# A Fourier layer on one core: partitions reordered by channel, its 32-point transforms on halves of the TensorE array

## The chip, the cores and the metric

The kernel runs on one core of one Trainium2 chip. The metric is the device time of one execution in microseconds. Before the change three runs took 3753.52, 3758.2 and 3759.49 us; the median, 3758.2 us, is the time that the change is measured against.

## What is computed

The network has four layers on an input of 4 images, 96 channels, 64 x 64 pixels: a Mamba block with a fusion, a ConvNeXt block, a linear attention with a quantized feed-forward part, and a Fourier mixing with another quantized feed-forward part. The change lies in the Fourier mixing of the fourth layer. For 4 images of 4096 tokens with 96 channels, normalized over the channels, it computes:

```python
h = jnp.einsum('bnc,hc->bnh', x, w1)
h = jax.nn.relu(_bn(h, bn1_gamma, bn1_beta, bn1_mean, bn1_var))
X = jnp.fft.fft(h, axis=1, norm='ortho')
xr = jax.nn.relu(X.real * rd - X.imag * idg + rb)
xi = jax.nn.relu(X.imag * rd + X.real * idg + ib)
y = jnp.fft.ifft(xr + 1j * xi, axis=1, norm='ortho').real
o = jnp.einsum('bnh,ch->bnc', y, w2)
return _bn(o, bn2_gamma, bn2_beta, bn2_mean, bn2_var)
```

`w1` widens 96 channels to 192, the transforms run over the 4096 tokens, `rd` and `idg` are one number per channel, and the caller adds the result to x. All of it is in float32.

## The kernel before

The token sum `t` (96 channels x 16384 tokens) stays in SBUF. The function `fourier` (L1285) splits a transform of 4096 tokens into 128 x 32: token = 32 a + n, with `N1` = 128 values of a and `N2` = 32 values of n. Since the input is real, only 65 of 128 frequencies over a are made (`K1` = 65).

The work is cut into 8 units (4 images, and the lower or upper 96 of the 192 channels), each unit into 4 iterations of 6 groups, a group being 4 channels. So there are 32 iterations (`its`), and a partition index of 128 stands for 32 values of n (or of a frequency) times the 4 channels of a group. Before the change the channel is the fast index of the two: partition = 4 n + channel.

The steps of iteration i, each a function:

- `w1` (L1319): two tokens n at a time, PE multiplies the normalized `h` (taken with a step of 32 tokens, that is 128 bytes) by the weights; ACT writes the result after ReLU into `hh` (L1328, 128x192 elements, in two halves).
- `over_n1` (L1334): PE makes the 128-point transform over a of six groups, with `hh` as stationary operand (L1340). DVE multiplies by the twiddle factors, twice (L1344, into `p0` and `p1`), POOL adds the products into real and imaginary part `f` (L1352, two additions on 128 partitions x 390 elements).
- `over_n2` (L1354): PE makes the 32-point transform over n with four matmuls of 390 columns (L1361 to L1364). The stationary operands are 128x128 matrices that are 32-point cosines and sines for each of the four channels; two matmuls add up in each of the PSUM tiles `xi` and `xr`. DVE multiplies `xi` by the coefficients (`ec`, L1367), ACT multiplies `xr` and adds the bias in twelve pieces (`av`, L1376), POOL adds and subtracts the two (L1379, L1380).
- `fold` (L1382): ReLU by ACT (L1386) and DVE, which also folds the frequencies k and 128 - k (L1391, and L1394 for frequency 64) into `zz`; ACT negates one part (L1397).
- `over_k2` (L1399): PE makes the 32-point transform back, with `zz` as stationary operand, twelve matmuls of 128 columns (L1409, L1410), three groups to a PSUM tile; ACT copies each of the two tiles into `bt` (L1411).
- `row64` (L1416): once per unit, the row of frequency 64, through DRAM into `bt`.
- `over_k1` (L1436) and `w2` (L1448): for a finished unit, per block of four n, PE makes the 128-point transform back (L1444), ACT copies it (`ys`, L1446), PE multiplies by the output weights (L1455), DVE adds the result to `t` (L1459, L1461).
- `norm1`, `norm2` (L1303, L1311): the channel norm of the next image.

The order on PE, DVE, ACT and POOL is the program order (`manual_schedule`, L1464): a loop over j (L1468) runs `over_n1(j)`, part of the norm or of `w1` of the next image, `fold(j-2)`, `over_k1` of a first block, `over_n2(j-1)`, `w2`, `over_k1` of a second block, `over_k2(j-3)`, and `w2`. Each engine takes its instructions in that order and waits for the semaphores of the others. So there are three kinds of iteration: with the norm (first half of an image's unit pair, for the next image), with `w1` (second half), and plain ones (last image). Output blocks start with j = 8. The small PSUM tiles `m` (two) are shared by `norm1`, `norm2`, `w1`, `over_k1`, `w2` and `row64` in turn; `s1`, `xr`, `xi` exist once, `i1` twice.

The constants are made on the host by `_constants` (L1550) and laid out by `_lay_out` (L1603), and loaded by `consts2` (L821) during an earlier layer.

Of the kernel before, what the change touches and what calls it, by code (L numbers as in the profile page):

```python
# [9 lines left out]
F32 = mybir.dt.float32  # L10
# [8 lines left out]
B, C, HW, L = 4, 96, 64, 4096  # L19
# [3 lines left out]
MB = 512  # L23
# [79 lines left out]
class Net:  # L103
# [717 lines left out]
    def consts2(self, wk, small):  # L821
# [81 lines left out]
        self.dft2 = load("dft2", [128, 3 * 128])  # L903
# [381 lines left out]
    def fourier(self, dram, t, h):  # L1285
# [5 lines left out]
        with ExitStack() as ctx:  # L1291
# [3 lines left out]
            nbs, bc, bs = (self.dft2[:, k * 128 : (k + 1) * 128] for k in range(3))  # L1295
# [23 lines left out]
            def w1(b, n):  # L1319

                if n == 0:
                    for half in range(2):
                        hh[2 * b + half] = wk.tile([N1, CG, N2, 4], F32, name="hh", tag="hh", bufs=3)
                ps = misc(N1)[:, : 4 * C].rearrange("p (n c) -> p n c", n=2)
                for d in range(2):
                    nc.tensor.matmul(ps[:, d, :], h[:, n + d :: N2], self.a_w1, start=True, stop=True)  # L1326
                for half in range(2):
                    nc.scalar.activation(  # L1328
                        hh[2 * b + half][:, :, n : n + 2, :].rearrange("p g n c -> p n g c"),
                        ps[:, :, half * C : (half + 1) * C].rearrange("p n (g c) -> p n g c", c=4),  # L1330
                        AF.Relu,
                    )

            def over_n1(i):  # L1334

                u, g = its[i]
                ps = pln.tile([128, 2, MB], F32, name="s1_ps", tag="s1")
                for d in range(G):
                    a = d % 3 * 2 * K1
                    nc.tensor.matmul(ps[:, d // 3, a : a + 2 * K1], hh[u][:, g + d], self.dft1, start=True, stop=True)  # L1340
                pp = []
                for k in range(2):
                    p = wk.tile([128, G, 2, K1], F32, name=f"p{k}", tag=f"p{k}")
                    nc.vector.tensor_mul(  # L1344
                        p.rearrange("p (a g) r k -> p a g (r k)", a=2),
                        ps[:, :, : 6 * K1].rearrange("p a (g k) -> p a g k", g=3),
                        self.twid[:, k : k + 1, None, :].to_broadcast([128, 2, 3, 2 * K1]),
                    )
                    pp.append(p)
                f[i] = wk.tile([128, 2, G, K1], F32, name="f", tag="f", bufs=2)  # L1350
                for r in range(2):
                    nc.gpsimd.tensor_add(f[i][:, r], pp[0][:, :, r, :], pp[1][:, :, 1 - r, :])  # L1352

            def over_n2(i):  # L1354
# [3 lines left out]
                fr, fi = (f[i][:, r].rearrange("p g k -> p (g k)") for r in range(2))  # L1358
                f.pop(i)
                xr, xi = (pln.tile([128, MB], F32, name=f"x{r}_ps", tag=f"x{r}")[:, : G * K1] for r in "ri")  # L1360
                nc.tensor.matmul(xi, bc, fi, start=True, stop=False)  # L1361
                nc.tensor.matmul(xi, nbs, fr, start=False, stop=True)
                nc.tensor.matmul(xr, bc, fr, start=True, stop=False)
                nc.tensor.matmul(xr, bs, fi, start=False, stop=True)  # L1364
# [34 lines left out]
            def over_k2(i):  # L1399

                u, g = its[i]
                z = zz.pop(i)
                if g == 0:
                    bt[u] = wk.tile([N1, N2, C], F32, name="bt", tag="bt", bufs=2)
                for e in range(0, G, 3):
                    ps = pln.tile([N1, 4, 128], F32, name="i1_ps", tag="i1", bufs=2)[:, :3]
                    for d in range(3):
                        zd = z[:, e + d].rearrange("p k m -> p (k m)")
                        nc.tensor.matmul(ps[:, d], zd[:, 64:], bc, start=True, stop=False)  # L1409
                        nc.tensor.matmul(ps[:, d], zd[:, :128], bs, start=False, stop=True)  # L1410
                    nc.scalar.copy(  # L1411
                        bt[u].rearrange("p n (g c) -> p g n c", c=4)[:, g + e : g + e + 3],
                        ps.rearrange("p g (n c) -> p g n c", c=4),
                    )
# [13 lines left out]
            def fetch(k):  # L1428

                g = wk.tile([N1, CG, N2, 4], F32, name="hh", tag="hh", bufs=3)  # L1430
                g = g.rearrange("p g n c -> p (g n c)")[:, : N2 // 2 * N1].rearrange("p (n a) -> p n a", n=N2 // 2)
# [16 lines left out]
            def w2(u, n, kept):  # L1448

                b, half = units[u]  # L1450
                if u < len(units) - 1:
                    ps = misc(C)
                else:
                    ps = pln.tile([N1, 4, 128], F32, name="i1_ps", tag="i1", bufs=2)[:C].rearrange("p n a -> p (n a)")
# [95 lines left out]
def _constants():  # L1550
# [9 lines left out]
    th = 2 * np.pi * np.outer(np.repeat(np.arange(N2), 4), k1) / L  # L1560
# [4 lines left out]
    eye = np.eye(4)  # L1565
    bc, bs = np.kron(np.cos(th), eye), np.kron(np.sin(th), eye)
    dft2 = np.concatenate([-bs, bc, bs], 1)

    th = np.pi * np.outer(2 * m + 1, m) / N2
    dft64 = np.stack([np.kron(np.cos(th), eye), np.kron(-np.sin(th), eye)], 1)  # L1570
# [12 lines left out]
        "dft2": dft2.astype(f32),  # L1583
        "dft64": dft64.astype(f32),
# [18 lines left out]
def _lay_out(i):  # L1603
# [20 lines left out]
    for k, v in (("rd", np.diagonal(a["r"])), ("id", np.diagonal(a["i"])), ("rb", a["rb"]), ("ib", a["ib"])):  # L1624
        v128[k] = np.tile(v.reshape(48, 4).T, (32, 1))
# [56 lines left out]
```

## Time and profile before

| | |
|---|---|
| median of three runs | 3758.2 us (3753.52 to 3759.49) |
| the profiled execution | 3750.98 us, its span 3749.2 us |
| granted TensorE clock, mean | 0.919 of full speed |
| PE busy (matmul) | 3115.1 us, 83% |
| PE weight loads | 1404.9 us, 37% |
| DVE busy | 2981.6 us, 80% |
| ACT busy | 2720.5 us, 73% |
| POOL busy | 2566.7 us, 68% |
| DMA moved | 446.63 MB |

The profile is of one execution. Its times count from the start of the span. PE stands for matmuls, PEld for weight loads, which overlap them; DVE is VectorE, ACT ScalarE, POOL GpSimd. A row of a group gives line, engine, operation, output and inputs with partitions x elements, count, busy time, the mean of one in ns, and the idle time ahead of it with what ended it. A float32 matmul appears as two records (two passes over the array), each with its own weight load. The ends of matmuls are modelled, so their starts are the better measure. In the timeline, a bracket behind a row is the engine's idle time ahead of it and the instruction that ended it. The chain of waits follows the work that ended last back from the end, at each step to what released it or to the instruction before it on its engine; "issue" in it is time in which the engine waited for nothing that the profile shows.

The Fourier layer lies between 3108.2 and 3616.2 us.

### The profile page before, as it was taken

Reading aid. Unit: us, or ns where it says so; the run is one execution under the profiler, and the core shown is the slowest. Engines: PE = TensorE matmul, PEld = TensorE weight load, DVE = VectorE, ACT = ScalarE, POOL = GpSimd, SP = SyncE. Lnnn points to the kernel's source line nnn. Section 1 sums busy time; section 2 is a strip of 40 time slices with the busy share of each in tenths; the row PEclk is TensorE's granted clock in tenths of the full one; section 3 lists DMA queues with packets and bytes.
Section 4 is the critical chain, followed back from the end, with each engine's and each line's share of the span. In section 5 each row is a group of like instructions: output and inputs, shape, how many; then the busy total and the mean of one; then the engine's idle time right before and its main releaser. Section 6 shows DMA issues by size and latency. Waiting matters only on the chain. (4 is left out here: it accounts for less than half of the span.)

```text
span 3749.2 us, 46836 instructions
## 1 busy us (share of the span) xinstructions
PE 3115.1 (83%) x15326; PEld 1404.9 (37%) x15326; DVE 2981.6 (80%) x2644; ACT 2720.5 (73%) x5456; POOL 2566.7 (68%) x922
## 2 busy tenths in 40 slices
PE   7887888788878887887888888657799997999888
PEld 3232223223222322232233233147344435676643
DVE  5999999999999999999999999931662493444649
ACT  6887888888888888888888888541345685656557
POOL 1899989898999899989989998811001174434527
PEclk8999899899989998999999899658899999999999
DMA  7656665666565666666665666376000000011001
GB/s 187 156 152 160 166 161 148 165 160 172 145 170 152 173 149 169 157 157 161 166 165 142 172 157 173 91 214 217 1 0 1 1 1 6 24 35 46 24 11 57
DMA packets 171644, 446.63 MB, mean 119 GB/s; under 512 B 48756, under 2 KB 50750, under 8 KB 168064
## 3 DMA queue, kind: packets, MB, share of 16 engines
q1 hardware_dynamic: 171400, 443.64, 45.7%
q8 instruction: 121, 1.98, 0.2%
q14 instruction: 123, 1.01, 0.1%
HBM read 369.97 MB, written 73.50 MB: 118 GB/s over the span
## 5 line engine op out<-in xcount | busy, mean ns | idle before, releaser
L648 POOL TENSOR_TENSOR hs<-hs,crep 128x2048 f32<-128x2048 f32 x384 | 1601.2, 4185 | 224.2 <-DVE hs L643 176.4
L610 ACT ACTIVATE da<-ddb,nega 128x1024 f32<-128x1024 f32 x576 | 661.5, 1149 | 197.7 <-DMA ddb<-dd 124.3
L643 DVE TENSOR_TENSOR_SCAN hs<-da,state,rep 128x1024 f32<-128x1024 f32 x288 | 669.2, 2338 | 39.6 <-PE rep L594 21.9
L621 POOL TENSOR_TENSOR up<-udb,brep 128x1024 f32<-128x1024 f32 x192 | 453.0, 2360 | 73.1 <-DMA udb<-ud 58.9
L665 PE MATMUL y<-hs,sel_r 128*32 128x512 f32 x3072 | 459.6, 692 | 12.8 <-POOL hs L648 12.3
L599 PE MATMUL rep<-dbl,sel_b 32*128 32x512 f32 x768 | 250.1, 730 | 215.1 <-DVE hs L643 215.0
L507 ACT ACTIVATE uta<-delta,bt 128x192 f32<-128x192 f32 x1024 | 381.1, 446 | 0.0
L287 PE MATMUL ps<-n,w_x 97*64 97x512 f32 x1536 | 353.8, 602 | 13.0 <-ACT xc L411 12.1
L643 DVE TENSOR_TENSOR_SCAN hs<-da,state,u 128x1024 f32<-128x1024 f32 x144 | 338.1, 2348 | 23.9 <-PE y L665 8.2
L643 DVE TENSOR_TENSOR_SCAN hs<-dap,state,up 128x1024 f32<-128x1024 f32 x144 | 335.2, 2328 | 0.5 <-ACT dap L610 0.5
L594 PE MATMUL rep<-ident,uta 128*128 128x128 f32 x1536 | 222.6, 287 | 105.6 <-DVE hs L643 93.2
L594 PEld LDWEIGHTS rep<-ident,uta 128*128 128x128 f32 x1536 | 174.9, 146 | 246.5 <-issue 133.3
L636 DVE TENSOR_TENSOR u<-udb,rep 128x1024 f32<-128x1024 f32 x192 | 235.4, 1226 | 24.8 <-DMA udb<-ud 11.4
L1240 POOL CAST hq<-y 128x1536 fp8e5<-128x1536 f16 x64 | 94.0, 1469 | 218.1 <-issue 122.6
L643 DVE TENSOR_TENSOR_SCAN hs<-da,rep 128x1024 f32<-128x1024 f32 x96 | 217.9, 2282 | 21.2 <-PE rep L594 14.8
L610 ACT ACTIVATE dap<-ddb,nega 128x1024 f32<-128x1024 f32 x192 | 214.8, 1119 | 24.9 <-DVE hs L643 24.4
L636 DVE TENSOR_TENSOR rep<-udb,rep 128x1024 f32<-128x1024 f32 x192 | 232.0, 1208 | 0.0
L287 PEld LDWEIGHTS ps<-n,w_x 97*64 97x64 f32 x1536 | 103.8, 137 | 260.2 <-issue 210.0
L665 PEld LDWEIGHTS y<-hs,sel_r 128*32 128x32 f32 x3072 | 73.7, 118 | 335.2 <-issue 257.7
L599 PEld LDWEIGHTS rep<-dbl,sel_b 32*128 32x128 f32 x768 | 65.8, 205 | 353.6 <-issue 295.2
L658 PE MATMUL y<-xc,dp 128*128 128x512 f32 x192 | 125.7, 743 | 31.3 <-ACT bt L463 31.3
L1379 POOL TENSOR_TENSOR av<-av,ec 128x780 f32<-128x780 f32 x32 | 58.8, 1837 | 133.7 <-ACT av L1376 133.7
(275 smaller groups left out, 6201.3 us busy)
## 6 DMA issues: line engine op xcount, KB each, us to landing
udb<-ud SPq DMA_DIRECT2D x768, 128.0 KB
ddb<-dd SPq DMA_DIRECT2D x768, 128.0 KB
crep<-cd SPq DMA_DIRECT2D x512, 128.0 KB
dd<-delta SPq DMA_DIRECT2D x64, 384.0 KB
band<-in_band SPq DMA_DIRECT2D x24, 1024.0 KB
ud<-delta SPq DMA_DIRECT2D x62, 384.0 KB
brep<-cd SPq DMA_DIRECT2D x128, 128.0 KB
x<-in_x SPq DMA_DIRECT2D x32, 384.0 KB
```

The source lines that it names most:

```text
L287: nc.tensor.matmul(ps[rows], w[:, 64 * p : 64 * p + 64], rhs[:, at.start + shift : at.stop + shift], start=k == 0, stop=k == len(ws) - 1, ...
L507: nc.scalar.mul(m["uta"][:, q, :, 32 * s4 : 32 * s4 + 32].rearrange("t (p j) d -> t p j d", p=3), m["udt"][:, :, q].rearrange("t p (j d) - ...
L594: nc.tensor.transpose(x[:, q * 128 : q * 128 + 128], made[k]["uta"][:, q, 2 * h + j], self.ident)
L599: nc.tensor.matmul(x[:, at], sel_b[rows, g], made[k]["dbl"][rows, at], start=True, stop=True)
L610: nc.scalar.activation(da, made[k]["dd", h, j], AF.Exp, scale=nega[:, col : col + 1])
L621: nc.gpsimd.tensor_mul(up, made[k]["ud", p][:, j], made[k]["brep", GP])
L636: nc.vector.tensor_mul(u, made[k]["ud", h][:, j], x)
L643: nc.vector.tensor_tensor_scan(hs[:, 1:], made[k].pop(("da", t)), u, st, ALU.mult, ALU.add)
L648: nc.gpsimd.tensor_mul(hs[:, :, :T], hs[:, :, 1:], twice(made[k]["crep", g]))
L658: nc.tensor.matmul(y, dp[:, items[k][2], p], made[k]["xc"][:, p], start=True, stop=True)
L665: nc.tensor.matmul(made[k]["y", p][row : row + 32], sel_r, made[k]["hs", p, g][:, j, at], start=False, stop=True, skip_group_check=True,)
L1240: nc.gpsimd.tensor_copy(q, y2, saturate=False)
```

## The change

Partitions are reordered: partition = 32 channel + n instead of 4 n + channel, in the twiddle factors, the coefficients per channel and all transform matrices; `hh` changes from (group, n, channel) to (group, channel, n). With that, the 64 partitions of a channel pair are adjacent. The additions that make `f` put, for each channel pair q, the real part on partitions 0 to 63 and the imaginary part on 64 to 127, so a single matmul of 128 rows and 64 columns makes a real or an imaginary result of a pair: the pair's two results go to the two halves of the output partitions. In `over_k2`, each channel pair is a matmul of 64 rows, and the two pairs write to two PSUM tiles.

```diff
-        self.dft2 = load("dft2", [128, 3 * 128])
+        self.dft2 = load("dft2", [128, 2, 64])
+        self.idft2 = load("idft2", [128, 2, 64])
...
-            nbs, bc, bs = (self.dft2[:, k * 128 : (k + 1) * 128] for k in range(3))
+            bc, bs = (self.idft2[:, k] for k in range(2))
+            parts = [slice(0, 64), slice(64, 128)]
...
-                        hh[2 * b + half] = wk.tile([N1, CG, N2, 4], F32, name="hh", tag="hh", bufs=3)
+                        hh[2 * b + half] = wk.tile([N1, CG, 4, N2], F32, name="hh", tag="hh", bufs=3)
...
                     nc.scalar.activation(
-                        hh[2 * b + half][:, :, n : n + 2, :].rearrange("p g n c -> p n g c"),
-                        ps[:, :, half * C : (half + 1) * C].rearrange("p n (g c) -> p n g c", c=4),
+                        hh[2 * b + half][:, :, :, n : n + 2].rearrange("p g c n -> p n (g c)"),
+                        ps[:, :, half * C : (half + 1) * C],
                         AF.Relu,
                     )
...
-                for r in range(2):
-                    nc.gpsimd.tensor_add(f[i][:, r], pp[0][:, :, r, :], pp[1][:, :, 1 - r, :])
+                for q, rows in enumerate(parts):
+                    for r in range(2):
+                        nc.gpsimd.tensor_add(f[i][parts[r], q], pp[0][rows, :, r, :], pp[1][rows, :, 1 - r, :])
...
-                fr, fi = (f[i][:, r].rearrange("p g k -> p (g k)") for r in range(2))
-                f.pop(i)
+                fs = f.pop(i).rearrange("p q g k -> p q (g k)")
                 xr, xi = (pln.tile([128, MB], F32, name=f"x{r}_ps", tag=f"x{r}")[:, : G * K1] for r in "ri")
-                nc.tensor.matmul(xi, bc, fi, start=True, stop=False)
-                nc.tensor.matmul(xi, nbs, fr, start=False, stop=True)
-                nc.tensor.matmul(xr, bc, fr, start=True, stop=False)
-                nc.tensor.matmul(xr, bs, fi, start=False, stop=True)
+                for r, x in ((1, xi), (0, xr)):
+                    for q, rows in enumerate(parts):
+                        nc.tensor.matmul(
+                            x[rows], self.dft2[:, r], fs[:, q], start=True, stop=True, skip_group_check=True
+                        )
...
-                for e in range(0, G, 3):
-                    ps = pln.tile([N1, 4, 128], F32, name="i1_ps", tag="i1", bufs=2)[:, :3]
-                    for d in range(3):
-                        zd = z[:, e + d].rearrange("p k m -> p (k m)")
-                        nc.tensor.matmul(ps[:, d], zd[:, 64:], bc, start=True, stop=False)
-                        nc.tensor.matmul(ps[:, d], zd[:, :128], bs, start=False, stop=True)
+                ps = [pln.tile([N1, MB], F32, name="i_ps", tag=f"i{q}") for q in range(2)]
+                for d in range(G):
+                    zd = z[:, d].rearrange("p k m -> p (k m)")
+                    for k, m in enumerate((bc, bs)):
+                        for p, rows in zip(ps, parts):
+                            nc.tensor.matmul(
+                                p[:, d * 64 : d * 64 + 64],
+                                zd[rows, 64 - 64 * k : 192 - 64 * k],
+                                m[rows],
+                                start=k == 0,
+                                stop=k == 1,
+                            )
+                for q, p in enumerate(ps):
                     nc.scalar.copy(
-                        bt[u].rearrange("p n (g c) -> p g n c", c=4)[:, g + e : g + e + 3],
-                        ps.rearrange("p g (n c) -> p g n c", c=4),
+                        bt[u].rearrange("p n (g c) -> p g n c", c=4)[:, g : g + G, :, 2 * q : 2 * q + 2],
+                        p[:, : G * 64].rearrange("p (g n c) -> p g n c", g=G, c=2),
                     )
...
-                    ps = pln.tile([N1, 4, 128], F32, name="i1_ps", tag="i1", bufs=2)[:C].rearrange("p n a -> p (n a)")
+                    ps = pln.tile([N1, MB], F32, name="i_ps", tag=f"i{n // 4 % 2}")[:C]
```

On the host the matrices follow the new order:

```diff
-    eye = np.eye(4)
-    bc, bs = np.kron(np.cos(th), eye), np.kron(np.sin(th), eye)
-    dft2 = np.concatenate([-bs, bc, bs], 1)
+    eye = np.eye(2)
+    dc, ds = np.kron(eye, np.cos(th)), np.kron(eye, np.sin(th))
+    dft2 = np.stack([np.concatenate([dc, ds]), np.concatenate([-ds, dc])], 1)
+    bc, bs = (np.tile((f(th)[None, :, :, None] * eye[:, None, None]).reshape(64, 64), (2, 1)) for f in (np.cos, np.sin))
+    idft2 = np.stack([bc, bs], 1)
```

## The prediction

> **What bounds the kernel now.** I read the page first (span 3749.2 us; the chain that ended last is mostly PE), then cut out the Fourier layer with the table by stretches, then followed its chain and its timeline. The layer runs from the first `w1` matmul at 3108.2 to the last addition at 3616.2 us, 508 us, 13.5% of the span; nothing else of the kernel is touched. In two stretches of it (columns: length; busy time and instructions of PE, PEld, DVE, ACT, POOL; TensorE clock; DMA):
>
> ```profile
> 3405.00:3471.00 66.00, 60.05 (x338) 47.97 (x337) 29.78 (x37) 38.89 (x111) 26.67 (x20) 1.00 0.16 49
> 3471.00:3554.00 83.00, 74.08 (x460) 55.98 (x460) 54.31 (x64) 46.75 (x128) 42.70 (x28) 1.00 0.09 27
> ```
>
> PE is the busiest engine at about 90%, yet one iteration of the late stretch is not a PE queue. The chain of waits through one of them (start, length, what):
>
> ```profile
> 3517.59 1.35 PE s_ps L1340 x12
> ...
> 3519.02 1.34 DVE p L1344 x2
> 3520.36 0.43 issue
> 3520.79 0.55 DVE zz L1391
> 3521.34 0.77 DVE z L1394
> 3522.11 0.48 DVE zz L1391
> ...
> 3522.61 0.52 ACT zz L1397
> 3523.13 0.48 ACT ys L1446
> ...
> 3523.65 1.10 PE m_ps L1455 x2
> ```
>
> PE's first transform releases DVE, DVE releases ACT, ACT's copy `ys` releases PE's L1455; then PE's own row of matmuls, `over_k1` (L1444) and `over_k2` (L1409, L1410, 2.68 us) among them, leads to the next L1340. `over_n2` (L1361 to L1364) is not in it: PE does it while DVE and ACT work, and then waits. The timeline has that wait (in brackets: idle time and releaser) in all three kinds of iteration: plain, with `w1`, with the norm:
>
> ```profile
> 3523.65 1.10 PE L1455 MATMUL m_ps<-ys,a_w2s 96*96 96x512 f32 x2 [1.23 <-ACT ys L1446]
> ...
> 3308.91 1.10 PE L1455 MATMUL m_ps<-ys,a_w2s 96*96 96x512 f32 x2 [0.68 <-ACT ys L1446]
> ...
> 3398.56 0.24 PEld L1306 LDWEIGHTS m_ps<-t,ones 96*96 96x96 f32 x2 [0.47 <-ACT ys L1446]
> ...
> 3410.58 2.73 DVE L1391 SCALAR_TENSOR_TENSOR zz<-av 128x384 f32<-128x384 f32 x1 [0.27 <-ACT av L1386]
> 3411.03 1.86 POOL L1352 TENSOR_TENSOR f<-p,p 128x390 f32<-128x390 f32 x2
> ```
>
> The last two lines show what lengthens the DVE part: an L1391 that takes 0.55 us alone took 2.73 us while POOL worked.
>
> **What the Trainium skill says.** (1) "SBUF — State Buffer", § SBUF: two separate sides: a DVE operation with two SBUF inputs and a GpSimd operation exclude one another for a whole instruction. The trace agrees: L1391 runs 0.55 us alone, 1.18 to 2.73 us beside POOL. (2) "TensorE: Matmul & The Clock Gate", § LDWEIGHTS: a weight load takes time by its columns, not its rows. The trace agrees: six loads of 128 columns for matmuls of one column (L836) came 0.112 us apart. (3) The same page, Part 3: matmuls on different row or column groups run at once. The trace agrees: L301's two row halves took 12 passes of 512 in six steps of 0.43 us, their loads two by two. (4) "TensorEngine Tiling (Array Packing)", § Key Properties: a change of tiling mode drains the array. The trace agrees: from the last stream of L684 to L301 and of L301 to L665 there are about 0.1 us, and the next load is then not hidden.
>
> ```profile
> 2544.96 0.75 PEld L836 LDWEIGHTS w_ps<-vec,c_w 96*128 96x128 f32 x6
> ```
>
> **The change, part by part** (per iteration; there are 32).
>
> *Transform over n2.* A matmul is two passes in this trace (64 records for 32 matmuls); eight passes of 390 columns start 0.328 us apart, 2.62 us. Now the same four matmuls go pairwise to the two column halves: four steps, 1.31 us, so 1.31 us less and 42 us of PE work over 32. On the path: nothing. PE then waits for `ys` 1.31 us longer than the 1.23, 0.68 and 0.47 us above, because `ys` hangs on DVE and ACT, which don't read this result before it; the two mode switches (0.2 us each) lie in the same gap. Only the four early iterations with `w1` and no output blocks (3184 to 3214 us) run PE without gaps; there ACT (its `av` and copies, then `hh`) is nearly as long. I take 0; bounds -5 and 0. If the cover were not there, it would be the full -42.
>
> *Transform over k2.* 24 passes of 128 columns at 0.111 us, 2.68 us, become 48 passes of 64 columns, two row halves at a time. The weights are still 128 columns wide, and L836 shows that a load bounds such a pass at 0.112 us however short the matmul: 24 pairs at 0.111 us, no gain. That two halves load at once I take from L599, which loads 128 columns on two row groups: two loads start within 0.01 us, the next two 0.11 us later. New is the mode switch: 0.1 us drain and 0.11 us of exposed load going in, 0.1 and 0.08 us going out, less 0.05 for the shorter last pass: 0.35 us (bounds 0.2 and 0.5; below nothing is excluded, since the load bound stays). It lies in the chain above in all iterations but the first: 31 x 0.35 = **11 us**.
>
> *POOL's additions.* Two on 128 partitions become four on 64. POOL costs by the row length: the 64-partition copies L964 and L965 on the two halves follow each other 1.07 us apart for 1024 elements and don't overlap.
>
> ```profile
> 2511.13 1.03 POOL L964 COPY x<-xt 64x1024 f32<-64x1024 f32 x1 [54.36 <-DVE xt L944]
> 2512.20 1.04 POOL L965 COPY x<-xt 64x1024 f32<-64x1024 f32 x1
> ```
>
> So four times 0.93 us (the pair L1352 takes 1.86), 1.86 us more, 60 us of POOL in all. POOL itself has the room (about half busy). What it costs is DVE's waits. In plain iterations the two L1391 are done with the second addition: 0. In iterations with the norm or with `w1` the additions come first (3394.49 to 3396.36 and 3305.01 to 3306.87) and L1391 at 3396.38 and 3306.10: the third addition now stands where L1391 ran. Least: DVE gets in between, and one addition (0.93) lies between the two L1391. Most: it waits for both, 1.86. I take 1.2, nearer the low end, as DVE mostly got in after one in the trace. Behind it wait L1397, `ys` and PE's L1455 or L1306. 16 such iterations with output blocks: **19 us**; the early eight, where less hangs on `ys`, 0.3 each: **2.5 us**. Below nothing only if POOL were faster on 64 partitions, which L964 excludes.
>
> *`hh` written with a step of 128 bytes.* The trace has no such ACT write. Bounds: 0, and what the same step costs others: L1326's loads 0.313 us against 0.191 (128 elements, 0.95 ns each), L1459 1.217 against 0.747 for L1043 (512 elements). At 0.95 ns, 192 elements add 0.18 us. I take that; two of the eight per iteration lie in the chain ahead of L1386 or L1455: 8 x 0.4 = **3 us**, and **1 us** in the sixteen `w1` before the loop, where ACT just passes PE's 0.9 us.
>
> *`bt` copies.* Still two of 384 elements, but both after the last pass, where one lay beside it: ACT is free there in plain iterations; 0.1 us in those with `w1`, 0.5 us before the last row: **1.5 us**. Writing two elements at a time instead of four: no row shows it; 0 to 0.2 us each, beside PE, taken at 0.
>
> *At no cost:* the constant `idft2` (one more DMA, 64 KB, long before it is used, in SP's queue of the layer before), other orders of constants and coefficients (same shapes), the L1340 loads (128 contiguous columns as before), PSUM banks (two of `i` as before).
>
> Sum: 11 + 19 + 2.5 + 3 + 1 + 1.5 = **38 us**. The profiled execution took 3750.98 us and would take 3789. The median of the runs shown is 3758.2, 7.2 above it; I put the same 38 on that: **3796 us**. Low ends: 31 x 0.2 + 16 x 0.93 - 5 = 16; high ends: 31 x 0.5 + 16 x 1.86 + 5 + 8 x 0.8 + 2 = 59. So 3774 to 3817.
>
> **The rivals.**
> *The n2 saving arrives (faster).* One mechanism: L1455 and L1306 follow `over_n2` directly in PE's queue, and if `ys` is there when n2 ends, each 1.31 us counts. For it: PE is 90% busy, and in norm iterations the chain even runs through L1361 to L1364. Against it: the three waits above, 0.47 us at the least. It decides once the DVE part gets shorter by the wait plus the saving, which nothing in the change does. Price, in the 24 norm and `w1` iterations: -31 + 11 = -20, 3738 us.
> *Row halves load one after the other (much slower).* Then 48 loads at 0.111 us, 2.67 us more, 31 times: +83 beside the 38, 3879 us. For it: loads bind this step, and all such pairs in the trace but L599's hide behind 512 columns. Against it: L599 itself.
> *Nothing to see.* POOL's additions on different partitions overlap, or DVE always wins: 11 us of switches less up to 5 of n2 remain, 3764 us. Against it: L964 and L965 in series, and the 2.73 us of L1391.
>
> **How the numbers follow.** Forecast (3774 to 3817) 0.68; nothing to see 0.14; serial loads 0.10; saving arrives 0.08. A measurement of this kernel can tell about 0.2%, 7.5 us, from no change. Slower 0.77 (forecast and serial loads, 0.78, less a little of the forecast's low end), same 0.15, faster 0.08. Leaving out serial loads and the faster case (0.18), the range is 3752 to 3820.
>
> **What would show it.** After: the layer's stretch about 38 us longer, everything before it unchanged. Right if n2's PE time is 1.31 us per iteration and PE's wait for `ys` grows; k2 stays at 2.7 us plus about 0.35 (5.3 would mean serial loads, 1.4 that loads don't bind); POOL has four 0.93 us additions, and L1391 or L1394 longer waits in norm and `w1` iterations; plain iterations go from 11.6 to about 11.95 us. Wrong if plain iterations become shorter, if 64-partition additions take half, or if `hh` writes take over 0.6 us a piece.

## The result, and the profile after

| | before | after |
|---|---|---|
| median of four runs | 3755.86 us (3749.58 to 3759.49) | 3813.43 us (3809.66 to 3816.36) |
| the profiled execution | 3750.98 us, span 3749.2 | 3816.36 us, span 3814.6 |
| granted TensorE clock, mean | 0.919 | 0.904 |
| PE busy, instructions | 3115.1 us, 15326 | 3152.5 us, 16094 |
| POOL busy, instructions | 2566.7 us, 922 | 2638.5 us, 986 |

The change makes the kernel slower: ratio 1.0155 (95% interval 1.0136 to 1.0173), 57.6 us between the medians, where the forecast had 38. The first `over_n1` starts at 3124.9 us (before: 3125.6), so nothing ahead of the layer's loop has moved. From there to the last `over_n1` it took 427.3 us before and takes 488.3 us now: 61.0 of the 65.4 us between the two spans were lost inside the loop, most of the rest right behind it. The added and moved lines shift the numbers: `over_n1` is L1342, POOL's additions L1355, `over_n2` L1365, the `zz` operations of DVE L1394 and L1397, `over_k2` L1413, `over_k1` L1454, `ys` L1456, `w2` L1465, `hh` L1330.

The table by stretches of the kernel after (columns as in the prediction), in the middle of the layer:

```profile
3290.00:3362.00 72.00, 61.89 (x388) 46.60 (x386) 31.71 (x35) 40.24 (x103) 34.47 (x26) 0.84 0.10 29
3510.00:3614.00 104.00, 87.23 (x691) 64.89 (x691) 54.84 (x65) 52.90 (x142) 59.21 (x44) 0.87 0.08 24
```

The sixth number after the length is the one that the forecast took as given: the granted clock is 0.84 and 0.87, where the stretches shown of before had 1.00. The timeline of two neighbouring plain iterations shows what that does:

```profile
3557.77 0.88 PE L1365 MATMUL xi_ps<-f,dft 128*64 128x390 f32 x4
...
3558.47 0.82 PE L1365 MATMUL xr_ps<-f,dft 128*64 128x390 f32 x4
...
3559.05 4.46 POOL L1355 TENSOR_TENSOR f<-p,p 64x390 f32<-64x390 f32 x4 [4.11 <-DVE p L1346]
...
3561.68 2.02 PE L1465 MATMUL m_ps<-ys,a_w2s 96*96 96x512 f32 x2 [2.38 <-ACT ys L1456]
...
3565.34 5.39 PE L1413 MATMUL i_ps<-idft,zz 64*128 64x64 f32 x48
...
3579.94 1.10 PE L1465 MATMUL m_ps<-ys,a_w2s 96*96 96x512 f32 x2 [2.39 <-ACT ys L1456]
...
3581.84 2.90 PE L1413 MATMUL i_ps<-idft,zz 64*128 64x64 f32 x48
```

`over_n2` has shrunk as forecast, to two times two steps, about 1.3 us, and PE's wait for `ys` has grown from 1.23 to 2.39 us. After the first of these waits the same instructions take twice as long: L1465 2.02 us instead of 1.10, `over_k2` 5.39 instead of 2.90. In the other two kinds of iteration the wait went from 0.68 to 2.31 us (`w1`) and from 0.47 to 1.71 us (norm):

```profile
3320.26 1.10 PE L1465 MATMUL m_ps<-ys,a_w2s 96*96 96x512 f32 x2 [2.31 <-ACT ys L1456]
...
3418.15 1.10 PE L1308 MATMUL m_ps<-t,ones 96*96 96x512 f32 x2 [1.71 <-ACT ys L1456]
```

The chain of waits through both iterations has the same links as before, those of PE in the slow one about twice as long:

```profile
3561.68 2.02 PE m_ps L1465 x2
3563.70 1.71 PE m_ps L1454 x8
3565.41 5.32 PE i_ps L1413 x48
3570.73 1.95 PE m_ps L1465 x2
3572.68 2.55 PE s_ps L1342 x12
...
3576.20 0.96 DVE p L1346
...
3577.62 0.77 DVE z L1397
...
3579.42 0.48 ACT ys L1456
...
3579.94 1.10 PE m_ps L1465 x2
3581.04 0.88 PE m_ps L1454 x8
3581.91 2.83 PE i_ps L1413 x48
```

Taken from one `over_n1` to the next, the seven plain iterations take 11.58 us (four), 11.93 and twice 12.29 us before. After, one takes 11.89, the other six 13.1 to 17.0. So there are two losses, and the second is not in the forecast: direct costs, and a lower clock that came with a longer gap.

### The profile page after: what moved, and what is told of

It reads as the page before. It is cut to its first block, busy times and chain, and to the rows that moved or that the text cites. A ratio compares the mean times of both kernels' runs of the same rounds, so it can differ in the third digit from the quotient of the medians.

```text
span 3814.6 us, 48448 instructions
## 1 busy us (share of the span) xinstructions
PE 3152.5 (83%) x16094; PEld 1413.3 (37%) x16094; DVE 3004.3 (79%) x2644; ACT 2736.8 (72%) x5456; POOL 2638.5 (69%) x986
## 3 DMA queue, kind: packets, MB, share of 16 engines
q14 instruction: 124, 1.02, 0.1%
## 5 line engine op out<-in xcount | busy, mean ns | idle before, releaser
L621 POOL TENSOR_TENSOR up<-udb,brep 128x1024 f32<-128x1024 f32 x192 | 453.6, 2363 | 78.4 <-DMA udb<-ud 62.3
L665 PE MATMUL y<-hs,sel_r 128*32 128x512 f32 x3072 | 464.5, 699 | 11.8 <-POOL hs L648 11.3
L643 DVE TENSOR_TENSOR_SCAN hs<-da,state,u 128x1024 f32<-128x1024 f32 x144 | 338.1, 2348 | 23.8 <-PE y L665 8.1
L1355 POOL TENSOR_TENSOR f<-p,p 64x390 f32<-64x390 f32 x128 | 137.2, 1072 | 149.0 <-DVE p L1346 142.3
L643 DVE TENSOR_TENSOR_SCAN hs<-da,rep 128x1024 f32<-128x1024 f32 x96 | 218.0, 2281 | 21.7 <-PE rep L594 15.7
```

Of the source, the lines that this page charges most:

```text
L621: nc.gpsimd.tensor_mul(up, made[k]["ud", p][:, j], made[k]["brep", GP])
L643: nc.vector.tensor_tensor_scan(hs[:, 1:], made[k].pop(("da", t)), u, st, ALU.mult, ALU.add)
L665: nc.tensor.matmul(made[k]["y", p][row : row + 32], sel_r, made[k]["hs", p, g][:, j, at], start=False, stop=True, skip_group_check=True,)
L1355: nc.gpsimd.tensor_add(f[i][parts[r], q], pp[0][rows, :, r, :], pp[1][rows, :, 1 - r, :])
```

## The experiments

**Clock theory:** about half of the loss is TensorE's clock, which falls because `over_n2` takes less and PE stands idle longer ahead of `w2`. **Rival (the forecast's own account):** the idle time costs nothing, and POOL's additions, DVE's waits and the mode switches cost it all.

All twelve runs in one table. The difference of medians is against the kernel before, run on the same chip (3748.65 to 3756.62 us). "Loop" is the distance from the first to the last `over_n1` in the profiled run, "half clock" the time in it at a granted clock of 0.5 (both from one execution of each kernel, where the medians are of four to fifteen).

| kernel | median us | to before | ratio, 95% | loop us | half clock us |
|---|---|---|---|---|---|
| before | | | | 427.3 | 17 |
| after | 3813.43 | +57.6 | 1.0136 to 1.0173 | 488.3 | 126 |
| e1 n2 doubled | 3761.26 | +12.6 | 1.0015 to 1.0049 | 450.1 | 31 |
| e2 only k2 changed | 3758.97 | +10.3 | 1.0020 to 1.0041 | 437.4 | 31 |
| e3 only n2 changed | 3785.09 | +36.4 | 1.0083 to 1.0118 | 464.5 | 96 |
| e4 before, half n2 | 3766.95 | +18.3 | 1.0030 to 1.0060 | 449.8 | 82 |
| e8 gap split | 3817.53 | +60.9 | 1.0147 to 1.0188 | 488.2 | 123 |
| e9 gap half filled | 3788.33 | +31.7 | 1.0062 to 1.0159 | 461.4 | 65 |
| e5 before, ys early | 3711.96 | -44.7 | 0.9866 to 0.9908 | 397.2 | 14 |
| e6 after, ys early | 3735.98 | -20.6 | 0.9933 to 0.9965 | 419.2 | 72 |
| e12 e5 with half n2 | 3682.41 | -67.5 | 0.9795 to 0.9838 | 374.4 | 31 |
| e11 before, POOL twice | 3777.08 | +27.2 | 1.0049 to 1.0090 | 453.6 | 34 |
| e7 e3 with ys early | 3709.43 | -40.5 | 0.9870 to 0.9914 | 396.9 | 31 |
| e10 mixture | 3714.22 | -35.7 | 0.9875 to 0.9927 | 399.9 | 17 |

**e1: give PE its work back.** To the kernel after:

```diff
-                for r, x in ((1, xi), (0, xr)):
+                for r, x in ((1, xi), (0, xr)) * 2:
```

> The changed kernel with over_n2's four matmuls issued twice, into the same tiles (the result is the same; PE gets back about 1.3 us of work per iteration, some 42 us in all, in the place where it now waits for ys). Clock theory: about 30 of the 57 us that the change cost come from a lower granted TensorE clock, and the clock falls because PE's gap ahead of L1465 grew to 2.3 to 3.1 us; with the gap filled again (back to 1.0 to 1.8 us) the clock in the layer goes back from 0.84-0.91 to about 0.97 and the time falls by about 30 us, to 3783 us, although PE does more. Rival (all of the cost is in POOL's four additions, DVE's waits and the mode switches; the clock is an accident): no gain, 3813 us; at most 42 us longer (3855) if the matmuls lie on the path.

There are 256 more matmul passes of 390 columns, and the loss falls from 57.6 to 12.6 us, 45 us less. Half-clock time falls from 126 to 31 us. Plain iterations take 11.89 us (twice 12.44), as long as in e2 below, where n2 is as before the change: the doubled work lies wholly in the gap, of which 1.08 us is left:

```profile
3509.49 1.10 PE L1465 MATMUL m_ps<-ys,a_w2s 96*96 96x512 f32 x2 [1.08 <-ACT ys L1456]
```

It came out lower than the 3783 us expected: the gap costs more than I had read off the periods. How much is known to about 10 us: 45 by the medians, 38 by the loops (488.3 less 450.1). In e1's trace the layers ahead of the loop, which do the same in both kernels, took 12 us less than in that of before, so its loop lost more than its total. Either way the rival is out: PE's idle time is not free here.

**e2 and e3: one half of the change each.** In e2 the additions and `over_n2` are as before the change, in the new order of partitions; in e3 `over_k2` is:

```diff
 e2
-                for q, rows in enumerate(parts):
-                    for r in range(2):
-                        nc.gpsimd.tensor_add(f[i][parts[r], q], pp[0][rows, :, r, :], pp[1][rows, :, 1 - r, :])
+                for r in range(2):
+                    nc.gpsimd.tensor_add(f[i][:, r], pp[0][:, :, r, :], pp[1][:, :, 1 - r, :])
...
+                nc.tensor.matmul(xi, fc, fi, start=True, stop=False)
...
 e3
+                        nc.tensor.matmul(ps[:, d], zd[:, 64:], bc, start=True, stop=False)
+                        nc.tensor.matmul(ps[:, d], zd[:, :128], bs, start=False, stop=True)
```

> The changed layout and over_k2 on row halves, but the additions (two on 128 partitions) and over_n2 (four 128x128 matmuls, 2.62 us) as before the change. Clock theory: PE's gap ahead of w2 stays at 0.5 to 1.2 us, the clock in the layer stays at about 0.97, and what is left is the mode switch in over_k2 (0.15 to 0.35 us, 31 times: 5 to 11 us) and the slower hh writes (3 to 10 us): 3768 us. Rival (the row halves are what costs the time, by switches or by the clock): 3795 to 3813 us.

> The changed layout with over_n2 on column halves and POOL's four additions, but over_k2 with 128-row matmuls and its two copies as before the change. Clock theory: the gap is there, the clock in the layer falls to 0.84-0.91, and only over_k2's switches (5 to 11 us) are saved against the changed kernel: 3805 us. Rival (the row halves are what costs the time): 3770 us and a clock near 0.97.

e2 costs 10.3 us and nearly keeps the clock (31 us at half); four of its plain iterations take 11.89 us where they took 11.58, 0.31 more (0.21 on the mean of seven). e3 costs 36.4 us and has 96 us at half clock. So most of the loss starts with n2; the row halves alone cost little. But e3 came out well below my 3805 us, and its half-clock time is 30 us less than that of the changed kernel: in it five of the seven plain iterations take 13.2 to 13.9 us and none 17.0. `over_k2` on row halves has a part in the clock, which its direct cost in e2 does not show; its traces are compared below, behind e4.

**e4: less work and nothing else.** The kernel before without the sine parts of the transform over n2:

```diff
-                nc.tensor.matmul(xi, bc, fi, start=True, stop=False)
-                nc.tensor.matmul(xi, nbs, fr, start=False, stop=True)
-                nc.tensor.matmul(xr, bc, fr, start=True, stop=False)
-                nc.tensor.matmul(xr, bs, fi, start=False, stop=True)
+                nc.tensor.matmul(xi, bc, fi, start=True, stop=True)
+                nc.tensor.matmul(xr, bc, fr, start=True, stop=True)
```

> The kernel before with two of over_n2's four matmuls left out (it leaves out the sine parts of the 32-point transform; POOL, DVE, ACT and over_k2 are untouched). It takes 1.31 us of PE work per iteration away, 42 us in all, as the change does, without its additions and mode switches. Clock theory: PE's gap grows to 1.8 to 2.5 us, the clock in the layer falls, and the kernel gets slower though it does less: about 3780 us. Rival (less PE work can only help or do nothing; the forecast's step): 3751 to 3756 us, clock as before.

It takes 42 us of PE work away and adds nothing, and is 18.3 us slower. Six of its seven plain iterations take 13.2 to 13.9 us instead of 11.58 to 12.29. Here the clock can be watched. The table by stretches of 3.4 us (PE busy is the first number after the length, the clock the sixth):

```profile
3530.92:3534.32 3.40, 1.10 (x4) 0.56 (x5) 3.00 (x4) 2.14 (x7) 2.10 (x2) 1.00 0.00 0
3534.34:3537.72 3.38, 3.38 (x18) 3.38 (x17) 1.13 (x1) 2.83 (x10) 0.94 (x1) 0.50 0.00 0
3537.76:3541.14 3.38, 3.38 (x27) 2.87 (x26) 0.72 (x1) 1.54 (x3) 2.68 (x2) 1.00 0.00 0
3541.16:3544.54 3.38, 2.75 (x18) 1.84 (x16) 3.15 (x5) 0.25 (x1) 0.73 (x1) 1.00 0.00 0
3544.58:3547.96 3.38, 1.52 (x8) 0.99 (x9) 2.95 (x5) 2.57 (x8) 1.66 (x2) 1.00 0.00 0
3548.00:3551.36 3.36, 3.36 (x18) 3.36 (x17) 0.72 (x1) 2.43 (x9) 1.37 (x1) 0.50 0.02 5
```

In this part of the program the clock changes on a fixed grid of about 3.41 us, and is 1.00 or 0.50 for a whole step. PE is busy 1.10 of 3.40 us, and the next step runs at half; busy 1.52 of 3.38, again; after 2.75 of 3.38 the clock stays. An iteration with one such step takes 1.65 us more, half a step. The Trainium skill ("TensorE: Matmul & The Clock Gate", Part 1, What's actually happening) describes such a free-running activity window of about 3.4 us, after which an idle array goes to half clock. This trace agrees with the window, but not with an idle window being needed: with the grid taken from the clock of each of the fourteen traces (3100 to 3690 us), of 1837 steps at full clock in which PE stood idle under 0.4 of the time 11 were followed by a step at half, of 111 with 0.55 or more 107, and between 0.45 and 0.55 44 of 72. Half a window idle, 1.7 us, is enough. Before, the gap of 1.23 us by itself cannot fill half a step; 2.39 us can.

**Why the changed kernel stays at half clock longer.** In e4 and e3 one step at half clock, sometimes two, follows a gap. In the loop of the changed kernel three to five come in a row six times, though PE is busy. Here is the slow iteration of the first timeline by steps (columns as in the prediction); then the time of `over_k2` (L1413) alone in the second to fourth of them (length; PE, PEld; clock; DMA); then a step of e3, where `over_k2` has 128 rows and takes most of the step too, and the step behind it:

```profile
3561.38:3564.78 3.40, 3.10 (x9) 1.96 (x10) 2.05 (x3) 3.40 (x13) 2.00 (x3) 0.50 0.38 158
3564.80:3568.18 3.38, 3.38 (x31) 3.10 (x30) 0.10 (x1) 0.95 (x3) 2.80 (x2) 0.50 0.01 2
3568.22:3571.60 3.38, 3.38 (x25) 2.71 (x24) 0.00 (x0) 0.84 (x3) 0.83 (x1) 0.50 0.00 0
3571.62:3575.01 3.39, 3.39 (x14) 2.87 (x13) 1.20 (x1) 0.75 (x1) 0.00 (x0) 0.50 0.00 0
3575.04:3578.42 3.38, 2.51 (x18) 1.32 (x16) 3.11 (x5) 0.00 (x0) 1.06 (x1) 1.00 0.00 0
```

```profile
3564.80:3568.18 3.38, 2.84 (x28) 2.84 (x28) 0.50 0.01 2
3568.22:3571.60 3.38, 2.51 (x24) 2.32 (x22) 0.50 0.00 0
3571.62:3575.01 3.39, 0.00 (x0) 0.00 (x0) 0.50 0.00 0
```

```profile
3566.04:3569.44 3.40, 3.40 (x19) 3.40 (x18) 0.69 (x1) 2.56 (x9) 1.63 (x2) 0.50 0.00 0
3569.46:3572.84 3.38, 3.38 (x26) 2.87 (x26) 1.19 (x1) 1.57 (x3) 2.25 (x2) 1.00 0.03 7
```

The two steps filled mostly by `over_k2` on row halves don't bring the clock back; the next, without it, does. Over all traces, of the steps at half clock in which PE was idle under 0.02: in the six kernels with row halves, 52 hold at least 1.0 us of `over_k2`, and none was followed by full clock, against 67 of the other 79. In the eight kernels with `over_k2` on 128 rows, 37 hold at least 1.0 us of it, and all were. At full clock the row halves start nothing: of 113 steps with 2 us or more of them none was followed by half. So the gap starts the half clock, and `over_k2` on row halves prolongs it. An estimate of its share: the loop of e3 is 23.8 us shorter than that of the changed kernel, and only 9.6 of that is what row halves cost directly (0.31 in 31 iterations), so some 14 of the 38 us need both. What of these matmuls keeps the clock down, the runs do not show.

**e8 and e9: what of the gap counts.** e8 puts a matmul of 64 columns into the middle of the gap; e9 doubles only the first half of n2:

```diff
 e8
                         over_n2(j - 1)
+                    if 2 <= j < len(its) + 1:
+                        ps = pln.tile([N1, MB], F32, name="i_ps", tag="i0")
+                        nc.tensor.matmul(ps[:64, :64], zz[j - 2][:, 0, 2], self.dft2[:, 0], start=True, stop=True)
 e9
-                for r, x in ((1, xi), (0, xr)):
+                for r, x in ((1, xi), (1, xi), (0, xr)):
```

> The changed kernel with one matmul of 64 columns (two passes, about 0.1 us; its result is not read) per iteration, which waits for the second DVE write of zz and so falls in the middle of PE's 2.4 us wait for ys and cuts it into pieces of about 1.3 and 1.0 us. Share theory (the clock of a stretch of 3.41 us is set by how much of the stretch before it PE stood idle, about half being enough): the idle share is hardly changed, so neither is the clock nor the time: about 3810 us. Length theory (the clock falls when one gap passes some 2 us): no gap passes 1.4 us, the clock goes back to about 0.97 and the time to 3783 us or less, as with n2 doubled.

> The changed kernel with only the first of over_n2's two halves issued twice: PE gets 0.66 us of work per iteration in the gap, half of what doubling gave, and the gap ahead of w2 goes from 2.4 to about 1.73 us in plain and w1 iterations. Share theory: a gap of 1.73 us is at the edge of half a stretch of 3.41 us and must fall wholly into one stretch to lower the clock, so nearly all stretches stay at full clock: about 3768 us, most of the gain of doubling. A theory in which the loss is proportional to the gap: half of the 52 us gained by doubling, 3787 us. Rival that the clock plays no part: 3813 us.

In e8 the gap is in two pieces, and L1465 still doubles:

```profile
3534.47 0.30 PE L1511 MATMUL i_ps<-dft,zz 128*64 128x64 f32 x2 [1.45 <-DVE zz L1394]
3535.40 1.96 PE L1465 MATMUL m_ps<-ys,a_w2s 96*96 96x512 f32 x2 [0.63 <-ACT ys L1456]
```

123 us at half clock and 3817.5 us: no gain. The seven plain iterations take 97.3 us in e8 as in the changed kernel. That the whole loop is as long too (488.2 against 488.3 us) is partly chance: norm iterations got 9.6 us shorter in all, since in them the gap of 1.70 us is at the edge and the added matmul fills 0.33 of it, and the early ones 14.1 longer, since there PE now waits for `zz` (2.3 to 5.1 us). The fourteen traces decide as e8's plain iterations do: of 14 steps at full clock with an idle share of 0.5 or more and no gap over 1.6 us all were followed by half clock (8 of them in e8); of 53 with a gap of 2.2 us or more, cut by the grid so that the share stayed under 0.4, 2 were. So it is the idle share, not the longest gap. e9 is a miss for my number: 3788, where I had expected 3768 from the share and 3787 from a loss proportional to the gap. Its trace is not proportional, though. Five of seven plain iterations take what they take in e1 (11.9 or 12.4 us) and lose nothing, the other two take 12.9 and 15.7. Its gap, in a fast iteration:

```profile
3527.03 1.10 PE L1465 MATMUL m_ps<-ys,a_w2s 96*96 96x512 f32 x2 [1.73 <-ACT ys L1456]
```

A gap of 1.73 us is at the edge of 1.7; whether it counts depends on where it falls on the grid, and it did more often than I thought; where it did, row halves could prolong it. The range of its runs, 3783.9 to 3816.0, fits that.

**e5 and e6: take the wait away instead.** `ys` stands on ACT behind L1397 (L1400 after), which waits for DVE. Moving that one line behind `over_k1` of the second block frees it, in the kernel before (e5) and after (e6):

```diff
-                nc.scalar.mul(z[:, :, 0], z[:, :, 2], -1.0)
+            def negate(i):
+                z = zz[i]
+                nc.scalar.mul(z[:, :, 0], z[:, :, 2], -1.0)
...
                         over_k1(*blocks[1], kept)
+                    if 2 <= j < len(its) + 2:
+                        negate(j - 2)
```

> The kernel before with one line moved: ACT's negation for zz (L1397) goes behind over_k1 of the second block, so that ACT copies ys of the first block as soon as PE has made it and PE does not wait ahead of w2. If that wait is on the path in every iteration, as the chain of waits says: 8 x 1.23 + 7 x 0.68 + 7 x 0.47 = 18 us less, about 3733 us (against 3749 to 3756). Rival (the loop over ACT, POOL and DVE, which av goes round, is as long as PE's queue, so something else waits in its place): no change, 3750 us.

> The changed kernel with the same line moved. Clock theory: without the gap the granted clock goes back to about 1, which gives some 30 us, and the waits of 2.4, 2.3 and 1.7 us go, another 8 x 2.4 + 7 x 2.3 + 7 x 1.7 = 47 us at most: 3735 us, so that n2's saving of 1.31 us per iteration arrives at last. Rival (POOL's four additions and DVE's waits hold the iteration, whatever PE does): no lower than 3780 us.

e5 runs at 3711.96 us, 1.1% faster than before, more than the 18 us expected. In it PE goes from n2 to `w2` without a wait:

```profile
3482.04 0.82 PE L1363 MATMUL xr_ps<-f,dft 128*128 128x390 f32 x2
3482.69 0.82 PE L1364 MATMUL xr_ps<-f,dft 128*128 128x390 f32 x2
3483.35 1.02 PE L1458 MATMUL m_ps<-ys,a_w2s 96*96 96x512 f32 x2
```

Plain iterations take 10.12 us (1.46 less), `w1` ones 0.9 less, norm ones only 0.1 less (the chain runs through other waits there); the rest came from early iterations, from those where norm and `w1` change over, and from after the last `over_n1`, none of which I had counted. e6 comes to 3735.98 us as expected, with plain iterations of 9.43 us: with the wait gone n2's saving arrives, 0.7 us net of the switches in `over_k2` and of what waits remain. But the clock did not go back to 1 as I had expected, and e6 is slower than e5: norm iterations are 0.6 us longer, and it still has 72 us at half clock, in the early iterations and the first norm or `w1` iteration of an image, in runs of up to four steps that hold `over_k2` on row halves.

**e12: the same cut with the wait gone.** e5 without the sine parts of n2, the edit of e4:

> The kernel before with ys copied early (L1397's negation moved) and with two of over_n2's four matmuls left out (it leaves out the sine parts of the 32-point transform). The same 1.31 us of PE work per iteration that made the kernel before slower when left out. If it was the wait for ys that swallowed the saving, and turned it into a lower clock, it must arrive now, in plain and w1 iterations at least: 15 to 31 times 1.31 us, 20 to 40 us below the 3712 us of the version with n2 whole: 3672 to 3692 us. Rival (less PE work lowers the clock wherever it is left out): 3712 us or more.

The cut that cost 18 us in e4 gains 23 us here (-67.5 against -44.7), 1.3 us in most norm and `w1` iterations and 1.0 in most plain ones, although half-clock time rises a little (31 us against 14 in e5). Whether PE's work counts is decided by the wait behind it.

**e11: POOL by itself.** To the kernel before:

```diff
-                for r in range(2):
+                for r in (0, 1) * 2:
```

> The kernel before with POOL's two additions made twice (the same values again), so that POOL takes four times 0.93 us as in the changed kernel, while PE's transforms, hh and k2 are as before. The forecast put 1.2 us per norm and w1 iteration and 2.5 us for the early ones on this, 21 us: 3776 us. Periods of the runs so far (n2 doubled against k2 alone) say 0.7 to 0.8 us per norm and w1 iteration and 0 in plain ones, some 12 to 15 us: 3768 us, the clock hardly lower since the gap ahead of w2 stays at 1.2 to 1.5 us. Rival (the additions cost nothing by themselves): 3752 to 3757 us.

27 us: the forecast's 21 was closer than my later 12 to 15, but not by its account. Plain iterations are unchanged at 11.58 us, six of the eight norm ones take 1.5 us more and six `w1` ones 0.7, 13 us together. Another 10 came in the first norm or `w1` iteration of each run of four, where half-clock time rose (34 us against 17 in the loop), and 3 in the early ones. And these additions have 128 partitions. The DVE rows of a norm iteration, kernel before, e11, and e1 (the changed kernel's additions, at full clock):

```profile
3380.41 0.56 DVE L1391 SCALAR_TENSOR_TENSOR zz<-av 128x384 f32<-128x384 f32 x1 [1.44 <-ACT av L1386]
3380.88 0.16 DVE L1394 SCALAR_TENSOR_TENSOR z<-av 128x6 f32<-128x6 f32 x1
```

```profile
3397.53 1.23 DVE L1391 SCALAR_TENSOR_TENSOR zz<-av 128x384 f32<-128x384 f32 x1 [1.44 <-ACT av L1386]
3398.69 0.98 DVE L1394 SCALAR_TENSOR_TENSOR z<-av 128x6 f32<-128x6 f32 x1
```

```profile
3380.42 0.56 DVE L1394 SCALAR_TENSOR_TENSOR zz<-av 128x384 f32<-128x384 f32 x1 [1.44 <-ACT av L1389]
3380.90 0.86 DVE L1397 SCALAR_TENSOR_TENSOR z<-av 128x6 f32<-128x6 f32 x1
```

In e11 both operations wait for POOL, 0.67 and 0.82 us. In e1 only the six-element one does, 0.70 us. That is 1.49 and 0.70 us ahead of the second `zz` write, which ACT and `ys` wait for, and the norm iterations grew by just that (1.5 us in those six, and 0.7 from e2 to e1). Why DVE gets in earlier beside four additions on 64 partitions is not settled.

**e7 and e10: can the change be kept?** e7 is e3 with `ys` early. e10 uses the column halves and four additions only where POOL's length delays nobody:

```diff
+            PLAIN = 24
...
+                if i < PLAIN:
+                    for r in range(2):
+                        nc.gpsimd.tensor_add(f[i][:, r], pp[0][:, :, r, :], pp[1][:, :, 1 - r, :])
+                else:
```

> The changed kernel's n2 on column halves and its four additions, over_k2 with 128-row matmuls as before, and ys copied early. Against the changed kernel with ys early (3736 us) only over_k2's mode switches go, 0.31 us in each of 31 iterations: 3726 us, plain iterations 9.1 us. Rival (what PE saves comes back as a wait and a lower clock): 3736 us or more.

> A mixture: layout of the changed kernel, over_k2 with 128-row matmuls, ys copied early; n2 on column halves with four additions only in the last eight iterations (plain ones, where POOL's longer additions delay nobody), in the others two additions on 128 partitions and four 128x128 matmuls. Against the kernel before with ys early (3712 us): 8 x 1.0 us less, some 3 us of slower hh writes more: 3707 us. Rival (the hh writes and the clock eat it): 3712 to 3720 us.

e7 gains 20 us on e6 where 10 were expected: without the row halves half-clock time goes from 72 to 31 us. The gain is in the norm, `w1` and early iterations; the seven plain ones, where three take the 9.1 us expected and four 9.8 to 10.5, take no less in all (67.9 us against 67.5). e10 is a miss: three of its plain iterations are 0.9 to 1.0 us shorter than e5's and the other four 0 to 0.3, 3.5 us in all where 8 were expected, and the `w1` ones are 0.6 longer; with `over_k2` and POOL as in e5, the `hh` writes are what is left there. e5, e7 and e10 (0.9887, 0.9892 and 0.9901) can't be told apart: with the wait gone n2 on column halves earns back what it costs, no more. All three beat both kernels, the one before by about 1%.

## Why the prediction was right or wrong, point by point

The differences of the loop to the kernel before, summed by kind of iteration (early: the first 8; norm 8; `w1` 8; plain 7), in us:

| | early | norm | w1 | plain | sum |
|---|---|---|---|---|---|
| e2: k2 and hh | 2.7 | 2.5 | 3.5 | 1.5 | 10.2 |
| e1: and POOL's four additions | 3.3 | 9.0 | 9.0 | 1.5 | 22.8 |
| after: and the longer gap | 3.3 | 19.9 | 23.4 | 14.5 | 61.0 |

- **n2: failed.** "On the path: nothing. PE then waits for `ys` 1.31 us longer" is right on the work and the wait (2.39 against 1.23 us), and wrong in the price. Nothing was saved and 38 us were lost (61.0 - 22.8; 45 by the medians), two thirds of the result or more, through the clock. The forecast had read the clock at 1.00 and treated it as given; here it followed from how PE's idle time lay. The bounds of -5 and 0 left no room for a loss. e1, e4 and e12 show it from three sides.
- **k2: right on the direct cost, incomplete.** 0.31 us an iteration (e2, four plain ones), 9.6 us in 31, against 0.35 and 11. Row halves load together: 2.90 us for the 48 passes at full clock. The 5.3 us that was to mean serial loads does occur, but at half clock, where these matmuls take twice as long: the sign was not as specific as I wrote. That row halves prolong half clock, some 14 of the 38 us, stands nowhere in the forecast.
- **POOL: right mechanism, size too large.** 12.6 us (22.8 - 10.2) instead of 21.5: 0.69 us per norm and 0.8 per `w1` iteration, below my least of 0.93, which assumed a whole addition between the two `zz` operations. It lies partly beside the first of them. 0 in plain iterations is confirmed. The additions follow one another, as forecast, 4.46 us for four where two took 2.44 in plain iterations before. The 12.6 rests on the loops; the medians of e1 and e2 differ by only 2.3 us, and in e1's trace the layers ahead of the loop were 8 us shorter than in e2's.
- **hh: right in size.** Two writes that took 0.55 us in the trace of before take 0.86: 0.16 us more each, forecast 0.18. On the path they cost 0.1 to 0.35 us per `w1` iteration in e2 (its difference less 0.31 for k2) and 0.6 in e10; the forecast had 0.4.
- **bt copies, constants: not measured by themselves.** L1421 is not in the chain shown, which is of plain iterations, where the forecast had 0.
- **The sum.** Direct costs 22.8 us where the forecast had 38, and 38 us of clock where it had none (12.6 and 45 by the medians; e1's loop also has 14 us more at half clock than that of before, so some of the 22.8 is clock too). The time fell into the range by luck, through two errors of opposite sign. The plain iteration's 11.95 us (11.89 at full clock) held in one of seven.
- **The rivals.** Nothing to see and serial loads are excluded. The saving does not arrive in this kernel, but does once the DVE part of the wait is off ACT's queue (e6, e12): the forecast had named that condition, and rightly said that nothing in the change meets it.

## What to carry to other kernels

Before a wait is counted as free cover, look at how much of a clock step of 3.41 us it leaves PE idle: here a gap of 1.2 us cost nothing and one of 2.4 us cost half a step of the following work, so less work made the kernel slower. Where the clock does fall, matmuls on row halves can hold it there, as `over_k2` did here. Where PE waits in every iteration, look first for what stands ahead of the awaited instruction in its engine's queue: moving one line on ACT brought 45 us, where leaving out half of n2 brought 23 at best (e12). A shorter operation on PE paid only once PE did not wait right behind it.

## What the runs showed of the hardware

- In the stretch of 3100 to 3690 us TensorE's clock is 1.00 or 0.50 for whole steps of about 3.41 us on a fixed grid. At full clock, a step with PE idle for 0.55 or more was followed by half clock in 107 of 111 cases, one under 0.4 in 11 of 1837. Cutting a gap of 2.4 us in plain iterations with a small matmul changed nothing (e8); filling it with 1.3 us of repeated work gained 45 us (e1).
- From a step at half clock in which PE was idle less than 0.02 of the time it went back to full in 164 of 235 cases, and in 1 of 59 with an idle share of 0.1 to 0.5: coming back takes more work than staying.
- It also depends on which work: of such busy steps with 1.0 us or more of `over_k2`, none of 52 brought full clock back where its matmuls have 64 rows and stream 64 columns, all of 37 did where they have 128 rows and stream 128.
- Four POOL additions on 64 partitions delayed DVE's `zz` part by 0.70 us, four on 128 partitions by 1.49 us, though one addition takes as long as the other (median 1.02 us on 64 partitions after and on 128 before).
